# Local attention layers: the turned keys are copied from PSUM by ScalarE instead of VectorE

## The chip, the cores and the metric

The kernel runs on one core of a Trainium2 chip. The core has five engines, each with its own instruction queue: TensorE (PE; its weight loads are shown as PEld and overlap the matmuls), VectorE (DVE), ScalarE (ACT), GpSimd (POOL) and SyncE (SP, which here issues the DMAs). An engine runs its queue in order; where it needs another engine's result it waits on a semaphore, and all that is queued behind the waiting instruction waits too. The metric is the device time of one execution in microseconds (us), lower is better.

## The reference

A two-block network on x[4, 1024, 128], all in fp32. Block 0 is a feature attention and a mixture of experts. Block 1 is a windowed attention with 16 heads, followed by two "local layers" (DEPTH 2, HEADS 8, DIM_HEAD 64, WINDOW 64). The change lies in the local layers:

```
def local_attention(q, k, v):                  # 8 heads of 64
    bq = q in windows of 64, times 8
    bk, bv = look_around(k), look_around(v)    # a window and the one before it: 128 keys
    sim = einsum('bhwid,bhwjd->bhwij', bq, bk)
    sim = where(mask, -max, sim)               # i < j, i > j + 64, before the start
    return einsum('bhwij,bhwjd->bhwid', softmax(sim), bv)

def _layer(x, wqkv, qs, ksc, wo, lg, lb, w1, b1, w2, b2):
    q, k, v = split(shift_token(x) @ wqkv)     # 3 x 512 columns
    q, k = l2norm(q) * qs, l2norm(k) * ksc
    q, k = rotary_xpos(q, k)
    x = x + local_attention(q, k, v) @ wo
    h = layernorm(shift_token(x)) * lg + lb
    a, g = split(h @ w1 + b1)                  # 2 x 341 columns
    return x + (a * gelu(g)) @ w2 + b2
```

## The kernel before

The local layers are cut into 64 tiles of 128 tokens: 2 layers, 4 batches, 8 tiles each; (l, b, t) names one. Activations are kept transposed (features on partitions). One loop over `g` (from -1 to 67) runs all 64 tiles as a software pipeline: an iteration works on several tiles at different stages. Its body in the order in which it is written, which is also TensorE's order, since the surrounding pool block schedules TensorE by hand (`manual_schedule` with PE alone):

1. `scores(g)`, L885: 32 small matmuls of the turned keys `kT` and queries `qT` into two PSUM tiles `s`. VectorE then applies mask, scale and row minimum for the eight heads (L892, "pr").
2. `project(g+2, 0)`, L653: the query product `qk` in PSUM. ScalarE squares it (`sq`, L656); VectorE makes `co` (L658), `si` (L663) and the square sums `ss` (L665); POOL adds `co` and `si` (L673).
3. `flip(g-2, 0)`, L926: the first half of the probabilities is transposed (`ptr`); ScalarE copies it out (`pt`, L928).
4. `over_sums(g-1)`: the probabilities are divided by their sums. VectorE takes the reciprocal of `sm` (L912); the product `pr` times `sm` is L919 on POOL for the first half of the heads, and L919 on VectorE for the second half. For the five tiles with (l, b) = (0, 0) and t from 3 on, called `light`, the second half is four activations on ScalarE (L917).
5. `project(g+2, 1)`: the same for the keys; POOL also makes the norms (L668, L669) and scales `co` by them (L675).
6. `flip(g-2, 1)`, and `exps(g)`: eight exponentials on ScalarE (L904), whose sums over a row are `sm`.
7. `turn(g+1, 0)`, L845 (L849 for light tiles): four transposes of the query's `co` into the PSUM tile `qktr`; ScalarE copies them out as `qT` (L852).
8. `outputs(g-3)`, L940: probabilities times values into the PSUM tile `o`; ScalarE copies it out (`os`, L944).
9. `turn(g+1, 1)`: the same transposes for the keys' `co`; VectorE copies them to `kT` (L858).
10. The first side step of the iteration, `values(g-1)` (L864, copied out by ScalarE as `vs`, L866), `project_out` in every fourth iteration (`yp`, L951; added up by VectorE, L952), and the other side steps.

The side steps are the MLP of an earlier half batch: `mlp_in` (transposes L972 and statistics), `mlp_out` (L160, `hn` L161 on ScalarE), `mlp_gate` (three products `gm` L986, Gelu on ScalarE L990), `mlp_up` (three products `a` L995, VectorE L997), `mlp_down` (`ym` L1003, VectorE L1004). They return with a period of four iterations: one with `mlp_down`, one with `project_out` and `mlp_out`, one with `mlp_gate`, one with `mlp_up` and the next `mlp_in`. Gelu and the exponential need different activation tables, so ScalarE loads a table (ACT_TABLE_LOAD, at L990 and L904) on each side of the gate.

PSUM has eight banks here: two for `s` (pool `pS`) and six (pool `pM`, tag "mid") that `qk`, `ptr`, `qktr`, `o`, `v`, `yp`, `gm`, `a`, `ym` and the rest take in turn. A tile that takes a bank waits until what read the bank's previous content is done, which may be an engine that has nothing to do with the tile itself.

The order of VectorE's, ScalarE's and POOL's instructions is not written by hand: the framework's scheduler decides it. `tc.issue_after(x)` (L911) keeps the instructions of its block behind instruction x in that order; in `over_sums` it names the `kT` copy that was issued last before it in the program.

Of the kernel before, what the change touches and what calls it, by code (L numbers as in the profile page):

```python
# [22 lines left out]
ALU = mybir.AluOpType  # L23
AX = mybir.AxisListType
PSUM = bass.MemoryType.PSUM

P = 128
# [21 lines left out]
def adaln_blocks(ctx: ExitStack, tc: tile.TileContext, a: dict, out: bass.AP):  # L49
    nc = tc.nc  # L50
    pe, act, dve, pool = nc.tensor, nc.scalar, nc.vector, nc.gpsimd
# [11 lines left out]
    def bc(ap, shape):  # L63

        return ap.unsqueeze(len(ap.shape)).to_broadcast(shape)
# [219 lines left out]
    with (  # L285
# [7 lines left out]
        kept = {}  # L293
# [306 lines left out]
    def const1(name, shape):  # L600
        return c1.tile(shape, F32, tag=name, name=name)

    wl = []
    for l in range(DEPTH):
        w = [const1(f"wqkv_{l}", [P, 3, HEADS * DH]), const1(f"wo_{l}", [P, 4, D]), const1(f"w1_{l}", [P, 2 * HID]), const1(f"w2_{l}", [P, 3, D])]
# [38 lines left out]
    late = {}  # L644
    pj = ctx.enter_context(tc.tile_pool(name="pj", bufs=3))

    def project(l, b, t, w, ps):


        nt = f"{l}_{b}_{t}_{w}"  # L650
        if w == 0:
            late[l, b, t, "ss"] = pj.tile([P, 2, HEADS], F32, tag="ss", name=f"ss_{nt}", bufs=4)
        pe.matmul(ps, lhsT=hs[l, b][:, t * P : (t + 1) * P], rhs=wl[l][0][:, w, :], start=True, stop=True)  # L653
        ph = ps.rearrange("p (h e) -> p h e", e=DH)
        sq = pj.tile([P, HEADS, DH], F32, tag="sq", name=f"sq_{nt}", bufs=2)
        act.activation(sq, ph, AF.Square)  # L656
        co = pj.tile([P, HEADS, DH], F32, tag=f"co{w}", name=f"co_{nt}")
        dve.tensor_tensor(co, ph, abs_[l][:, 0, t, w, :].unsqueeze(1).to_broadcast([P, HEADS, DH]), ALU.mult)  # L658
        si = pj.tile([P, HEADS, DH], F32, tag="si", name=f"si_{nt}", bufs=3)

        ex = bass.AP(tensor=ps.tensor, offset=ps.offset + 32, ap=[ps.ap[0], [DH, HEADS], [-32, 2], [1, 32]])
        sn = abs_[l][:, 1, t, w, :].rearrange("p (i e) -> p i e", i=2).unsqueeze(1).to_broadcast([P, HEADS, 2, 32])
        dve.tensor_tensor(si.rearrange("p h (i e) -> p h i e", i=2), ex, sn, ALU.mult)  # L663
        ss = late[l, b, t, "ss"]
        dve.tensor_reduce(ss[:, w, :], sq, AX.X, ALU.add)  # L665
        if w == 1:

            pool.tensor_scalar(ss, ss, 1.0e-24, None, ALU.max)  # L668
            pool.tensor_tensor(ss, ss, nhalf[:, 0:2].unsqueeze(2).to_broadcast([P, 2, HEADS]), ALU.pow)  # L669
        if w == 0 and light(l, b, t):  # L670
            late[l, b, t, "si"] = si
        else:
            pool.tensor_tensor(co, co, si, ALU.add)  # L673
        if w == 1:
            pool.tensor_tensor(co, co, bc(ss[:, 1, :], [P, HEADS, DH]), ALU.mult)  # L675
        late[l, b, t, "co", w] = co

    def light(l, b, t):

        return (l, b) == (0, 0) and t >= EARLY  # L680
# [5 lines left out]
    with (  # L686
# [107 lines left out]
        for g in range(-1, NG8 + 2):  # L794
            b, t = divmod(g, NT)
            ahead = 0 <= b and b + 1 < B
            if g == -1:
                weights(0, 0)
            when(g + 2, scores)
            when(g + 2, weights)  # L800
            if ahead and t in (2, 4):
                queries(b + 1, t // 2 - 1)
            for after, k, f in ((6, 0, tokens), (8, 0, normed), (11, 1, tokens), (13, 1, normed)):
                if (g - after) % NT == 0 and 0 <= (g - after) // NT < B - 1:
                    f((g - after) // NT, k, "h3")
            for at, k, f in ((1, 0, tokens), (3, 0, normed), (5, 1, tokens), (7, 1, normed)):
                if g == at:
                    f(B - 1, k, "h2")
            when(g - 1, back)
            when(g + 1, flip, (0, 1))  # L810
            when(g + 1, values)
            when(g, outputs)
            when(g + 1, flip, (2, 3))
            if t == 5 and 0 < b <= DEPTH:
                rotary(tab, abs_[b - 1], b - 1)
            if g % 4 == 1 and g > 4:
                project_out((g - 5) // NT, (g - 5) % NT // 4)
            if ahead and t in (3, 5):
                keys(b + 1, t // 2 - 1)

            for i, w in ((0, 0), (0, 1), (1, 0), (1, 1), (2, 0), (2, 1))[max(0, g - NG8 + 6) : max(0, g - NG8 + 7)]:
                project(0, 0, i, w, ps.tile([P, BLK], F32, tag="t", name=f"qk_0_0_{i}_{w}", bufs=2))
# [6 lines left out]
    with (  # L829
# [6 lines left out]
        kept = late  # L836

        def turn(l, b, t, w):
            nt = f"{l}_{b}_{t}_{w}"
            co = kept.pop((l, b, t, "co", w)).rearrange("p h e -> p (h e)")  # L840
            tp = pM.tile([P, 4, P], F32, tag="mid", name=f"qktr_{nt}")
            si = kept.pop((l, b, t, "si"), None) if w == 0 else None
            for i in range(4):
                if si is None:
                    pe.transpose(tp[:, i, :], co[:, i * P : (i + 1) * P], ident)  # L845
                else:

                    for j, x in enumerate((co, si.rearrange("p h e -> p (h e)"))):
                        pe.matmul(tp[:, i, :], lhsT=x[:, i * P : (i + 1) * P], rhs=ident, start=(j == 0), stop=(j == 1))  # L849
            if w == 0:  # L850
                kept[l, b, t, "q"] = wp.tile([P, 4, P], F32, tag="qT", name=f"qT_{nt}")
                act.copy(kept[l, b, t, "q"], tp)  # L852
                return
            if t == 0:

                kept[l, b, "k"] = wb.tile([P, 4, 64 + N], F32, tag="kT", name=f"kT_{nt}", bufs=1)
                pool.memset(kept[l, b, "k"][:, :, 0:64], 0.0)
            kept["copied"] = dve.tensor_copy(kept[l, b, "k"][:, :, 64 + t * P : 64 + (t + 1) * P], tp)  # L858

        def values(l, b, t):  # L860

# [45 lines left out]
        def over_sums(l, b, t):  # L907

            sm = kept.pop((l, b, t, "sm"))

            with tc.issue_after(kept["copied"].ins):  # L911
                dve.reciprocal(sm, sm)  # L912
                for j, eng in ((0, pool), (1, act if light(l, b, t) else dve)):
                    pr, _ = kept[l, b, t, "pr", j]
                    if eng is act:
                        for c in range(4):
                            act.activation(pr[:, c, :], pr[:, c, :], AF.Identity, scale=sm[:, j, c : c + 1])  # L917
                    else:
                        eng.tensor_tensor(pr, pr, bc(sm[:, j, :], [P, 4, P]), ALU.mult)  # L919
# [140 lines left out]
        def project_mid(l, b, t, w):  # L1060
            if (l, b) != (0, 0) or t >= EARLY:
                project(l, b, t, w, pM.tile([P, BLK], F32, tag="mid", name=f"qk_{l}_{b}_{t}_{w}"))

        for g in range(-1, tiles + 4):
# [5 lines left out]
            if 1 < g < NT - 1:  # L1070
                when(g + 1, turn, 0)
            when(g - 2, flip, 0)
            when(g - 1, over_sums)
            when(g + 2, project_mid, 1)
            when(g - 2, flip, 1)
            when(g, exps)
            for i in turns:
                if not 1 < g < NT - 1:
                    when(i, turn, 0)
                if i < EARLY and g < EARLY:  # L1080
                    when(i, turn, 1)
# [142 lines left out]
```

## Time and profile before

| what | value |
|---|---|
| time, median of 3 runs | 1245.24 us (1244.97, 1245.24, 1251.0) |
| the profiled execution | 1246.33 us, span 1244.5 us, granted TensorE clock 0.983 |
| `kT` copy, VectorE L858 | 64 of 128x512, median 0.679 us, from 580.4 to 1189.3 us |
| `qT` copy, ScalarE L852 | 64 of 128x512, median 0.577 us |
| normalising product L919 | POOL 64, median 1.042 us; VectorE 59, median 0.725 us |
| L917 on ScalarE | 20 of 128x128, median 0.390 us, from 609.8 to 644.3 us |
| reciprocal L912, VectorE | 64, median 0.186 us |
| who waits for the `kT` copy | PEld `v` L864 12.1 us in 13 waits; PEld `s` L885 6.3 us in 5; PE `s` L885 6.1 us in 16 |

The local layers' score matmuls run from 581 to 1193 us of the span; what lies before belongs to the other blocks. A line of the timeline gives start, duration, engine, source line, operation, output and inputs; the bracket at its end is how long the engine stood idle before it and which instruction ended that. The waits are summed by the waiting line and the line that ended them: us in total, times, longest. A PEld wait is one of a weight load, which can lie beside matmuls that still run; a PE wait is one of the matmul itself.

### The profile page before, as it was taken

How to read it: one execution, taken by the hardware profiler on the slowest of the kernel's cores; microseconds unless marked ns; L12 is line 12 of the kernel's file. 1: busy time of each engine (PE TensorE's matmuls, PEld its weight loads, DVE VectorE, ACT ScalarE, POOL GpSimd, SP SyncE). 2: the span in 40 equal slices, each digit the busy share in tenths (PEclk: the TensorE clock that was granted, in tenths of full speed). 3: DMA queues.
4: the chain of work that ended last, by engine and by line, in shares of the span. 5: the costliest groups of instructions: out<-in, count | busy, mean ns of one | idle time of the engine just before them, and what ended most of it. 6: DMA issues, size and time to landing. Idle time of an engine off the chain costs nothing.

```text
span 1244.5 us, 34772 instructions
## 1 busy us (share of the span) xinstructions
PE 1162.8 (93%) x13578; PEld 714.7 (57%) x13578; DVE 878.8 (71%) x2798; ACT 817.8 (66%) x2223; POOL 823.3 (66%) x813
## 2 busy tenths in 40 slices
PE   6789999999899999988898999999999999999998
PEld 5644453534476667755665556665555556565564
DVE  5556263452476667666878988898898888998864
ACT  3363373322577677766886788788877887788862
POOL 4436445746334445444889988888899889888840
PEclk8699999999999999999999999999999999999999
DMA  6040404021400000000112111111111111111110
GB/s 179 1 130 8 138 0 132 7 74 63 137 4 4 3 20 14 11 3 3 35 27 48 27 35 26 32 40 27 39 28 34 39 29 45 38 27 31 36 40 26
DMA packets 36136, 51.04 MB, mean 41 GB/s; under 512 B 5850, under 2 KB 17668, under 8 KB 35844
## 3 DMA queue, kind: packets, MB, share of 16 engines
q1 hardware_dynamic: 35540, 48.29, 14.1%
q8 instruction: 107, 1.75, 0.6%
q10 hardware_dynamic: 432, 0.53, 0.1%
q14 instruction: 57, 0.47, 0.1%
HBM read 26.52 MB, written 2.36 MB: 23 GB/s over the span
## 4 chain that ended last, share of the span: by engine, by line
PE 43%; DVE 27%; ACT 18%; POOL 7%; issue 5%; DMA 1%; POOLq 0%; ACTq 0%; SPq 0%; DVEq 0%
ACT pr L904 5%; PE h L489 4%; PE yp L951 4%; DVE pr L892 3%; DVE co L658 3%; PE s L885 3%; DVE si L663 3%; DVE ss L665 3%; PE ptr L735 3%; PE qk L653 3%; POOL u L494 2%; ACT sq L656 2%; PE s L261 2%; PE obank L752 2%; DVE ge L997 2%
## 5 line engine op out<-in xcount | busy, mean ns | idle before, releaser
L904 ACT ACTIVATE pr<-pr,mx 128x128 f32<-128x128 f32 x512 | 200.8, 403 | 88.2 <-DVE mx L892 88.1
L673 POOL TENSOR_TENSOR co<-co,si 128x512 f32<-128x512 f32 x123 | 156.7, 1280 | 79.5 <-DVE si L663 72.2
L669 POOL TENSOR_TENSOR ss<-ss,nhalf 128x16 f32<-128x16 f32 x64 | 191.7, 2995 | 5.3
L892 DVE CUSTOM_DVE_ANT_0 pr<-s,masks,ss 128x128 f32<-128x128 f32 x512 | 144.2, 342 | 42.4 <-PE s L885 42.0
L653 PE MATMUL qk<-wqkv,hs 128*128 128x512 f32 x256 | 137.7, 620 | 4.9 <-ACT pt L737 4.9
L494 POOL TENSOR_TENSOR u<-u,cw 128x512 f32<-128x512 f32 x64 | 81.1, 1271 | 74.4 <-ACT u L492 74.4
L489 PE MATMUL h<-hT,w 128*128 128x512 f32 x256 | 123.8, 605 | 4.0 <-DVE g L496 4.0
L496 DVE TENSOR_TENSOR g<-u,h 128x512 f32<-128x512 f32 x64 | 43.8, 686 | 114.9 <-POOL u L494 114.9
L279 DVE TENSOR_REDUCE mx<-s 128x4 f32<-128x448 f32 x128 | 73.5, 617 | 56.4 <-PE s L270 56.4
L658 DVE TENSOR_TENSOR co<-qk,ab 128x512 f32<-128x512 f32 x128 | 86.7, 677 | 26.0 <-ACT sq L656 26.0
L904 ACT ACTIVATION_READ_ACCUMULATOR pr<-pr,mx 128x1 f32 x512 | 101.7, 199 | 0.0
L492 ACT ACTIVATE u<-h 128x512 f32<-128x512 f32 x64 | 38.2, 598 | 93.2 <-PE h L489 85.7
L926 PEld LDWEIGHTS ptr<-ident,pr 128*128 128x128 f32 x512 | 63.5, 141 | 61.6 <-issue 54.8
L663 DVE TENSOR_TENSOR si<-qk,ab 128x512 f32<-128x512 f32 x128 | 86.8, 678 | 0.0
L489 PEld LDWEIGHTS h<-hT,w 128*128 128x128 f32 x256 | 48.3, 194 | 66.2 <-issue 51.0
L665 DVE TENSOR_REDUCE ss<-sq 128x8 f32<-128x512 f32 x128 | 86.2, 673 | 0.0
L656 ACT ACTIVATE sq<-qk 128x512 f32<-128x512 f32 x128 | 74.9, 586 | 14.8 <-PE qk L653 12.3
L845 PE MATMUL qktr<-ident,co 128*128 128x128 f32 x492 | 76.9, 280 | 6.6 <-POOL co L675 5.3
L885 PEld LDWEIGHTS s<-kT,qT 64*64 64x64 f32 x2048 | 56.8, 134 | 45.6 <-issue 22.1
L919 POOL TENSOR_TENSOR pr<-pr,sm 128x512 f32<-128x512 f32 x64 | 74.7, 1168 | 7.9 <-DVE sm L912 7.9
L885 PE MATMUL s<-kT,qT 64*64 64x128 f32 x2048 | 72.1, 277 | 7.6 <-DVE kT L858 6.1
L737 ACT COPY pt<-ptr 112x512 f32<-112x512 f32 x128 | 72.5, 612 | 8.6 <-PE ptr L735 8.6
(212 smaller groups left out, 2871.2 us busy)
## 6 DMA issues: line engine op xcount, KB each, us to landing
cw<-cd SPq DMA_DIRECT2D x128, 128.0 KB, 3.0
ve<-vs SPq DMA_DIRECT2D x120, 128.0 KB, 2.3
hs<-hT SPq DMA_DIRECT2D x16, 256.0 KB, 3.2
out<-out SPq DMA_DIRECT2D x7, 256.0 KB, 2.7
xin<-in_x SPq DMA_DIRECT2D x3, 512.0 KB, 6.1
w<-in_w SPq DMA_DIRECT2D x3, 512.0 KB, 5.0
wqkv<-in_wqkv SPq DMA_DIRECT2D x2, 768.0 KB, 5.3
ab<-in_tab SPq DMA_DIRECT2D x1, 1024.0 KB, 7.3
```

The source lines that it names most:

```text
L489: pe.matmul(h, lhsT=w[:, c * P : (c + 1) * P], rhs=hT[b][:, blk(k)], start=True, stop=True)
L494: pool.tensor_tensor(u, u, kept[b, k, "cw"][:, c, :], ALU.mult)
L653: pe.matmul(ps, lhsT=hs[l, b][:, t * P : (t + 1) * P], rhs=wl[l][0][:, w, :], start=True, stop=True)
L656: act.activation(sq, ph, AF.Square)
L658: dve.tensor_tensor(co, ph, abs_[l][:, 0, t, w, :].unsqueeze(1).to_broadcast([P, HEADS, DH]), ALU.mult)
L663: dve.tensor_tensor(si.rearrange("p h (i e) -> p h i e", i=2), ex, sn, ALU.mult)
L665: dve.tensor_reduce(ss[:, w, :], sq, AX.X, ALU.add)
L669: pool.tensor_tensor(ss, ss, nhalf[:, 0:2].unsqueeze(2).to_broadcast([P, 2, HEADS]), ALU.pow)
L673: pool.tensor_tensor(co, co, si, ALU.add)
L885: pe.matmul(S[j][qs, c, :], lhsT=q[rw, c, qs], rhs=k[rw, c, at : at + P], start=True, stop=True)
L892: dve.tensor_tensor_reduce(out=pr[:, c, :], in0=S[j][:, c, :], in1=mk[:, min(t, 1), :], scale=kept[l, b, t, "ss"][:, 0, h : h + 1], scalar ...
L904: act.activation(pr[:, c, :], pr[:, c, :], AF.Exp, bias=mx[:, j, c : c + 1], scale=-1.0, accum_out=sm[:, j, c : c + 1])
```

## The change

Three lines change. The keys' copy from PSUM goes from VectorE to ScalarE, in all 64 tiles. It was also the instruction behind which `over_sums` was kept; that place is taken by the last square sum (L665) that `project` issued before it in the program. In the loop body `over_sums(g-1)` follows `project(g+2, 0)`, so that is the query's square sum of the same iteration, where before it was the `kT` copy of the iteration before. Nothing of what is computed changes.

```
@@ project
         ss = late[l, b, t, "ss"]
-        dve.tensor_reduce(ss[:, w, :], sq, AX.X, ALU.add)
+        late["summed"] = dve.tensor_reduce(ss[:, w, :], sq, AX.X, ALU.add)
@@ turn
-            kept["copied"] = dve.tensor_copy(kept[l, b, "k"][:, :, 64 + t * P : 64 + (t + 1) * P], tp)
+            act.copy(kept[l, b, "k"][:, :, 64 + t * P : 64 + (t + 1) * P], tp)
@@ over_sums
-            with tc.issue_after(kept["copied"].ins):
+            with tc.issue_after(kept["summed"].ins):
```

(`kept` and `late` are the same dictionary.)

## The prediction

> **What bounds the kernel now.** I read the busy times first, then stretches of the steady part, then its waits, then single iterations.
>
> ```profile
> PE 1162.8 (93%) x13578; PEld 714.7 (57%) x13578; DVE 878.8 (71%) x2798; ACT 817.8 (66%) x2223; POOL 823.3 (66%) x813
> ```
>
> The window view of one stretch of the local layers (start:end, length, then busy us and instructions of PE, PEld, DVE, ACT, POOL, then clock, DMA share, GB/s):
>
> ```profile
> 800.00:900.00 100.00, 99.38 (x957) 59.86 (x955) 83.98 (x290) 79.88 (x243) 86.73 (x71) 1.00 0.15 36
> ```
>
> TensorE leaves 0.62 us of 100 open, so whatever makes it wait lengthens the kernel, and there is little waiting to take away. The local layers run in a cycle of four iterations of 39.84 us (score groups start at 784.4, 794.1, 804.8, 814.2 and 824.2); I name them by their side step: D (down), P (project_out), G (gate), U (up and mlp_in). From about 682 to 1200 us there are 13 cycles. The waits between 700 and 1180 us that touch the change:
>
> ```profile
> PEld v L864 <- DVE kT L858: 11.1, 12, 1.0
> DVE co L658 <- ACT sq L656: 9.6, 12, 1.0
> PEld a L995 <- DVE si L663: 6.8, 12, 0.6
> ...
> PE s L885 <- DVE kT L858: 2.8, 11, 0.3
> ```
>
> Each comes once a cycle. Two name the copy that moves; the third says that in U the last up product's weights already wait for VectorE's `si`, so anything put ahead of that `si` is paid in full. The iteration U, from the timeline (start, us, engine, line):
>
> ```profile
> 811.45 0.58 ACT L852 COPY qT<-qktr 128x512 f32<-128x512 f32 x1
> 811.91 0.59 ACT L944 COPY os<-o 128x512 f32<-128x512 f32 x1
> 812.52 1.28 ACT L990 ACT_TABLE_LOAD   x1
> ...
> 818.45 0.69 DVE L658 TENSOR_TENSOR co<-qk,ab 128x512 f32<-128x512 f32 x1 [0.78 <-ACT sq L656]
> ...
> 821.58 0.28 PEld L995 LDWEIGHTS a<-hn,w 128*85 128x85 f32 x2 [0.54 <-DVE si L663]
> ...
> 822.04 0.68 DVE L858 COPY kT<-qktr 128x512 f32<-128x512 f32 x1
> 822.77 0.30 PEld L864 LDWEIGHTS v<-wqkv,hs 128*128 128x128 f32 x2 [0.91 <-DVE kT L858]
> ```
>
> ScalarE runs from `os` at 811.91 through the table load, three Gelus, `vs`, the second table load and the first exponential to the square at 817.84 without a pause; VectorE stands idle 0.78 us for that square, then runs six products and sums and `kT`. So U hangs on ScalarE, then VectorE, then TensorE.
>
> **The change part by part.** It takes 64 copies of 0.678 us off VectorE (43.4 us busy) and adds 64 to ScalarE, which I price by the same shape and PSUM source there, `qT` L852: 0.576 us each, 0.47 from its start to the next (811.45 to 811.91). The changed program's own instruction order then says where the rest goes. The ScalarE copy stands behind `os`, and ahead of the table load in G. The reciprocal L912 moves up behind the first square sum of an iteration, and VectorE's normalising product L919 behind the second `co`: both ahead of the second `si`. POOL's L919 moves behind the first `co` sum. In D that order exists already and gives the prices:
>
> ```profile
> 790.74 0.18 DVE L912 RECIPROCAL sm<-sm 128x8 f32<-128x8 f32 x1
> 790.85 0.63 DVE L658 TENSOR_TENSOR co<-qk,ab 128x512 f32<-128x512 f32 x1
> 791.40 0.78 DVE L919 TENSOR_TENSOR pr<-pr,sm 128x512 f32<-128x512 f32 x1
> ...
> 792.11 0.68 DVE L663 TENSOR_TENSOR si<-qk,ab 128x512 f32<-128x512 f32 x1
> ```
>
> Start to start, the reciprocal takes 0.11 and the product 0.71.
>
> *U, a loss.* The copy in G pushes ScalarE's solid run by 0.47, so U's square and VectorE's first product come 0.47 later; the reciprocal and L919 add 0.82 ahead of the second `si`. That `si` (820.85, 0.68 long) ends 0.47+0.82 = 1.29 later, at 822.81 in place of 821.52, and the last up product's weights, 0.06 behind it today, go from 821.58 to 822.87. Its matmuls were not late today (0.43 is a pass, weights at 820.41 and 820.84; 819.98 plus four of them is 821.70, 0.12 after the weight load); the `v` matmul behind them was, by 0.21 (819.98 plus six of 0.43 is 822.56, and it ran at 822.77, when `kT` was done). So `v`, `mlp_in` and the next scores come 1.29-0.21 = 1.07 later (rounded rows). Times 13: +13.9. Bounds: 0.61 (8 us) if the 0.47 on ScalarE finds cover, 1.29 (17 us) if `v` then finds another wait of its own. I take 1.07 because every piece has its own row. Behind `v` stands all of the next iteration, so nothing hides it. `kT` itself ends on ScalarE at about 824.4 (`os` 823.4, copy 823.9), ahead of scores due 825.3.
>
> *D, a gain.* The scores' wait for `kT` (0.29 at 794.12) goes: ScalarE's `os` begins at 791.96, its copy ends near 793.0, and scores can't start before `v` is through at 793.83 or so. Worth 0.25 (2.8 us over 11 waits), times 13: -3.3. Bounds 0 and -0.29.
>
> *P, a small loss.* After the change project_out's PSUM tile waits for `qT` in place of VectorE's work; `qT` runs from 800.80 to 801.38 and the first matmul L951 runs at 801.25 today. If only the matmul waits it is 0.13, if its weights (0.19) wait too some 0.34: I take 0.25, as today's wait there stands on the weights. Times 13: +3.3, bounds +1.7 and +4.4.
>
> *G, nothing.* Its PSUM tiles wait for the first `si` (809.51), `qT` (812.03) and `os` (812.50), each before its use (810.62, 812.34, 813.20); `kT` near 813.0 is before scores at 814.15.
>
> *The first batch, a loss.* For five tiles ("light") the second half of the product is four ScalarE activations L917. Today they lie in a gap:
>
> ```profile
> 616.76 0.58 ACT L944 COPY os<-o 128x512 f32<-128x512 f32 x1
> 617.86 0.59 ACT L866 COPY vs<-v 128x512 f32<-128x512 f32 x1 [0.52 <-PE v L864]
> 618.34 1.28 ACT L917 ACTIVATE pr<-pr,sm 128x128 f32<-128x128 f32 x4
> ```
>
> After the change they stand amid the exponentials, ahead of `os` and `kT`. There the loop is scores at 609.62, first exponential 1.66 later, `os` 5.48 after that. With 1.28 more, 0.47 to the copy, 0.58 of copy and 0.05 to scores it is 9.52 against 8.56: +0.96 for three iterations, +2.9. The iterations around it, by the same sums, give -0.3, +1.5, +0.4 and about -0.7: +0.9. Bounds for the batch: 0 (the four hide in a VectorE wait) to +6.
>
> The relief of VectorE elsewhere buys nothing: its 84 of 100 us leave slack that TensorE (99.4) sets. Nor does a DMA move.
>
> The sum: 13.9-3.3+3.3+3.8 = +17.7. The profiled run took 1246.33 (span 1244.5), 1.1 over the median; on the median 1245.24 that is 1263. All low ends: 8-3.8+1.7+0 = +6; all high: 17+0+4.4+6 = +27.
>
> The Trainium skill (Perfetto Trace Analysis, Identifying the Most-Contended Engine) speaks for the change: for engines other than TensorE occupancy is a fair measure, and the fullest is to be relieved first. By that VectorE, above ScalarE in the window view, should be unloaded, and if all 43.4 us counted the kernel would take some 1202, an estimate. The rows above go against it, since in U VectorE waits for ScalarE.
>
> **The rivals.** (1) Not slower: the copy's waits on TensorE are all that counts, and the moved 0.82 is covered by VectorE's 0.78 idle before U's first product. Place: U. It decides if the second `si` ends no more than some 0.1 later than now (matmuls due 821.70). Then 13 times 0.21+0.25 is won, 6.0, and 1.7 lost in P: 1241. Against it: the built order puts the moved pair behind that idle time. (2) Little change: U's lateness only replaces the 0.21, D's gain pays P, and the first batch's 3.8 stays: 1249. For it speaks the 0.91 that the `v` weights wait today; against it that this is weight time, of which only 0.21 reaches the matmul. (3) POOL turns late: its L919 (1.04) behind the `co` sum holds up the chain to L675, whose result is at 798.77 for a turn at 799.46 in P. 1.04-0.69 = 0.35 times 13 is 4.6 more: 1267. Against it: POOL takes the same work and in D this order today.
>
> **How the numbers follow.** Forecast 0.62, rival 1 0.13, rival 2 0.17, rival 3 0.08. The time is the forecast's, 1263; its own range, the sums of low and of high ends, is 1251 to 1272. For 8 in 10 it reaches down over rival 2 and leaves out rival 1 and the top, where all high ends would have to meet: 1247 to 1270. A change under 0.5% (6.2 us: 1239 to 1251.5) can't be told from none. Faster: half of rival 1, 0.07. Same: the other half and most of rival 2, 0.18. Slower: 0.75.
>
> **What would show it.** In the profile after: `a` L995 waiting for `si` some 1.3 to 1.8 us in U, not 0.54; no wait of scores for `kT` in D; the cycle 39.84 growing to about 40.9; `yp` waiting for `qT`; periods of 9.5 in place of 8.56 near 610 to 635; VectorE's busy time down by 43. Wrong if U's second `si` isn't late, or if scores wait for ScalarE's `kT` in the steady part.

## The result and the profile after

The changed kernel takes 1258.74 us (median of 6 runs, 1254.94 to 1261.91) against 1245.58 us for the kernel before (6 runs, 1244.14 to 1251.0): a ratio of 1.0098, 95% interval [1.0072, 1.0123]. That is slower by some 12 to 13 us, about 1%, and clear of the 0.5% that the forecast used as its bound. The profiled run took 1258.30 us, span 1256.5, clock 0.983 as before.

The busy times of the kernel after:

```profile
PE 1168.4 (93%) x13578; PEld 714.8 (57%) x13578; DVE 847.1 (67%) x2734; ACT 847.5 (67%) x2287; POOL 822.5 (65%) x813
```

The window view from 800 to 900 us of the kernel after, columns as in the prediction:

```profile
800.00:900.00 100.00, 98.66 (x932) 58.47 (x934) 78.59 (x277) 82.30 (x254) 86.28 (x71) 1.00 0.14 32
```

VectorE lost 31.7 us of work and ScalarE gained 29.7; the engines are now level at 847, and the kernel is slower. The place to look is what TensorE waits for. The waits of the kernel after between 700 and 1180 us (waiting line, what ended the wait: us in total, times, longest):

```profile
PEld a L995 <- DVE si L663: 20.8, 24, 1.4
...
DVE co L658 <- ACT sq L656: 15.0, 12, 1.3
...
PEld yp L951 <- ACT qT L852: 9.4, 12, 0.9
...
PE a L995 <- DVE si L663: 6.6, 12, 0.6
PEld v L864 <- ACT qT L852: 6.2, 12, 0.6
```

The scores' wait for `kT` is gone, as forecast. In its place the weights of the up products wait for `si` three times as long as before (20.8 against 6.8), and now the matmul itself waits too (6.6), VectorE waits longer for the square (15.0 against 9.6), and `yp` and `v` wait for `qT`. The cycle of four iterations grew from 39.8 to 40.6 us (40.9 was forecast).

Period of each iteration, from one score group's first matmul to the next one's (median of 11 cycles), of all kernels of this study; "light" is the middle one of the three light iterations, and "layers" the time from the first score group to the last. Each ratio is that to runs of the kernel before taken alongside:

| kernel | D | P | G | U | light | layers | ratio to before, 95% interval |
|---|---|---|---|---|---|---|---|
| before | 9.67 | 10.66 | 9.37 | 10.08 | 8.57 | 610.97 | |
| after | 9.37 | 10.93 | 9.37 | 10.96 | 9.42 | 625.03 | 1.0098 [1.0072, 1.0123] |
| move_only | 10.05 | 10.91 | 9.37 | 10.49 | 8.57 | 625.15 | 1.0092 [1.0055, 1.0128] |
| copy_only | 9.37 | 10.66 | 9.37 | 10.86 | 8.26 | 615.60 | 1.0035 [1.0010, 1.0060] |
| copy_u_and_d | 9.37 | 10.66 | 9.37 | 10.38 | 8.26 | 609.54 | 0.9997 [0.9976, 1.0017] |
| light_as_before | 9.37 | 10.93 | 9.37 | 10.97 | 8.26 | 621.06 | 1.0072 [1.0051, 1.0094] |
| g_copy_on_vectore | 9.37 | 10.92 | 9.37 | 10.47 | 9.42 | 618.21 | one run |
| after_q_early | 9.37 | 11.09 | 9.37 | 10.38 | 9.42 | 620.27 | 1.0085 [1.0057, 1.0114] |
| before_q_early | 9.87 | 10.66 | 9.37 | 9.80 | 8.57 | 607.67 | 0.9961 [0.9943, 0.9979] |
| u_and_d_q_early | 9.37 | 10.79 | 9.37 | 9.89 | 8.26 | 604.00 | 0.9944 [0.9918, 0.9969] |
| d_only_q_early | 9.37 | 11.01 | 9.37 | 9.78 | 8.57 | 606.01 | 0.9949 [0.9929, 0.9968] |
| d_and_first_q_early | 9.37 | 11.01 | 9.37 | 9.79 | 8.26 | 605.32 | 0.9946 [0.9923, 0.9969] |
| copy_all_q_early | 9.37 | 10.78 | 9.37 | 10.36 | 8.26 | 610.51 | 1.0003 [0.9980, 1.0025] |

Between before and after the layers differ by 14.06 us; the spans differ by 12.0, because the first score group began 2.09 earlier in the profile after. That start lay anywhere from 575.9 to 581.4 us in these thirteen profiles, in which each engine runs the same instructions in the same order up to 570 us, so it is scatter from one execution to the next, and the column "layers" shows an effect of 1 us better than one run's time does.

### The profile page after: what moved, and what is told of

It reads as the page before. It is cut to its first block, busy times and chain, and to the rows that moved or that the text cites. A ratio compares the mean times of both kernels' runs of the same rounds, so it can differ in the third digit from the quotient of the medians.

```text
span 1256.5 us, 34784 instructions
## 1 busy us (share of the span) xinstructions
PE 1168.4 (93%) x13578; PEld 714.8 (57%) x13578; DVE 847.1 (67%) x2734; ACT 847.5 (67%) x2287; POOL 822.5 (65%) x813
## 4 chain that ended last, share of the span: by engine, by line
PE 58%; ACT 15%; DVE 15%; POOL 7%; issue 5%; DMA 1%; POOLq 0%; ACTq 0%; SPq 0%; DVEq 0%
PE qk L653 5%; PE yp L951 5%; PE h L489 5%; PE s L885 4%; PE v L864 3%; PE gm L986 3%; PE o L940 3%; PE qktr L845 3%; PE ptr L735 3%; PE ym L1003 3%; ACT pr L904 3%; PE ptr L926 2%; PE s L261 2%; POOL u L494 2%; ACT ge L990 2%
## 5 line engine op out<-in xcount | busy, mean ns | idle before, releaser
L673 POOL TENSOR_TENSOR co<-co,si 128x512 f32<-128x512 f32 x123 | 156.7, 1274 | 86.9 <-DVE si L663 83.6
L669 POOL TENSOR_TENSOR ss<-ss,nhalf 128x16 f32<-128x16 f32 x64 | 187.1, 2924 | 5.3
L919 POOL TENSOR_TENSOR pr<-pr,sm 128x512 f32<-128x512 f32 x64 | 88.0, 1375 | 16.4 <-DVE sm L912 12.0
L665 DVE TENSOR_REDUCE ss<-sq 128x8 f32<-128x512 f32 x128 | 86.1, 672 | 0.0
```

## The experiments

"The pair" is the reciprocal L912 with the normalising products behind it (L919, in light tiles also L917). Of each edit the lines that matter are shown; `[...]` and `(...)` stand for what did not change, and where only new lines stand, they replace the line of the same purpose.

### The two halves of the change apart

*move_only*: the order of the pair changes, the copy stays on VectorE (edit of the changed kernel).

```
-            act.copy(kept[l, b, "k"][...], tp)
+            dve.tensor_copy(kept[l, b, "k"][...], tp)
```

> VectorE keeps the keys' copy; only the reciprocal and the normalising products are moved ahead of the second si, as in the changed kernel. Theory (the moved pair is most of the loss): in U the second si ends 0.71 later (the pair's spacing measured in the changed kernel), the copy behind it too, so v waits for the copy and the period of U grows by 0.6 to 0.7 and that of P by 0.1 to 0.3 (yp behind the later si); D and G as before; the three light iterations stay near 8.6, since ScalarE's os is later but the copy on VectorE is not. Sum over 13 cycles some +9 to +12: 1255 to 1258 against 1245.5. Rival (the copy on ScalarE is the loss, the moved pair is covered by VectorE's idle time): U at 10.08, 1245 to 1247.

Measured: 1257.67 us (6 runs), the layers as long as with the whole change. U grew by 0.41, less than the 0.6 to 0.7 expected, P by 0.25, and D by 0.38, which no theory had: the time lies in the expected 1255 to 1258 only because D, and 1.4 us in the first batch, made up for what U lacked. The three largest waits of TensorE's matmuls (700 to 1180 us):

```profile
PE a L995 <- DVE si L663: 5.6, 12, 0.5
PE s L885 <- DVE kT L858: 3.6, 6, 0.6
PE s L885 <- ACT vs L866: 3.3, 5, 0.7
```

The moved pair alone makes the up products wait for `si`, and D's scores wait longer for `kT` and `vs`. It is no free part of the change. `v` does not wait for the copy here, as the theory had it: its weights and those of `yp` wait for `qT` (6.2 and 10.3 us, 12 waits each).

*copy_only*: ScalarE copies, the pair stays behind the copy (edit of the kernel before).

```
-            kept["copied"] = dve.tensor_copy(kept[l, b, "k"][...], tp)
+            kept["copied"] = act.copy(kept[l, b, "k"][...], tp)
```

> ScalarE makes the keys' copy in all 64 tiles; the reciprocal and products stay behind that copy, as before the change. Theory: U has only the 0.47 of the copy ahead of the gate's table load and no longer waits for VectorE's copy, so its period is 10.1 to 10.3 (before 10.08, changed 10.89); D loses 0.3 (9.37), P gains 0.25 (10.92), G 9.37; the light iterations fall to 8.3 to 8.6 (changed 9.42). Sum +0 to +4: 1245 to 1249. Open: in U VectorE's product now stands behind the statistics and could delay the next row minima in D by up to 0.7. Rival (ScalarE's copy is the loss): U near 10.9, 1256 or more.

Measured: 1248.37 us (10 runs). D, G and the light iterations as expected, but U 10.86, where 10.1 to 10.3 was expected, and P unchanged at 10.66, where +0.25 was expected. The timeline of U in this kernel says why (start, us, engine, line):

```profile
817.66 0.68 DVE L663 TENSOR_TENSOR si<-qk,ab 128x512 f32<-128x512 f32 x1
...
819.26 0.58 ACT L852 COPY qT<-qktr 128x512 f32<-128x512 f32 x1
...
819.89 1.13 PE L864 MATMUL v<-wqkv,hs 128*128 128x512 f32 x2 [0.40 <-ACT qT L852]
```

The second `si` is done at 818.34, in good time; what `v` waits for is `qT`, which ScalarE copies only behind all its exponentials. `v` reads nothing of `qT`, so what it waits for is its PSUM bank. By the waits, in the kernel before `v` took the bank that VectorE's `kT` copy frees; here it takes the one that `qT` frees. (The profile shows the waits, not the bank numbers.) Nobody wrote that: no edit names a bank, yet the engine that `v` or `yp` waits for changes from kernel to kernel. With `yp` in P it is the other way round: after the change it takes `qT`'s bank, here it keeps the one that `si` frees (2.9 us in 12 waits of its weights), and P stays at 10.66.

### The copy where it gains, and the price of the bank

*copy_u_and_d*: as copy_only, in U and D alone.

```
+            to = act.copy if t % 4 >= 2 else dve.tensor_copy
+            kept["copied"] = to(kept[l, b, "k"][...], tp)
```

> ScalarE makes the copy only in the iterations U and D (tiles with t mod 4 of 2 and 3), VectorE in P and G; the pair stays behind the copy as before. Theory: nothing is put ahead of the gate's table load and nothing ahead of si, so U falls by its 0.2 wait for the copy (9.9), D by 0.3 (9.37), P (10.66) and G (9.37) stay: 13 times -0.5, some 1239. If VectorE's product behind the statistics in U delays D's row minima and with them D's exponentials and outputs, D grows by up to 0.7 and the sum is 1245 to 1249. Rival (any copy on ScalarE costs): over 1250.

Measured: 1244.52 us (10 runs), no difference from the kernel before that can be told. D gained its 0.30; U lost 0.30 where a gain was expected, although nothing is ahead of the table load or of `si` here. `v` waits 4.0 us in 11 matmuls for `qT` in this kernel too. Up to `v`, TensorE, the squares and both `si` in U run as in the kernel before, to within 0.02 us; there `kT` is done 8.57 us after the scores, here `qT` at 8.87. So 0.30 is the price of the bank alone.

*g_copy_on_vectore*: the changed kernel, G's copy back on VectorE.

```
+            to = dve.tensor_copy if t % 4 == 1 else act.copy
+            to(kept[l, b, "k"][...], tp)
```

> The changed kernel with the copy of iteration G left on VectorE, so that ScalarE's table load in G is not pushed. Theory: U's square, qT and si come 0.47 earlier, the pair alone is left ahead of the second si, v some 9.1 after the scores: U 10.4 to 10.5 in place of 10.89; D, P and G as in the changed kernel (9.37, 10.92, 9.37). Some 5 us less than the changed kernel. Rival (the pair alone makes U's loss): U stays near 10.9.

Measured in a single run (1248.46 us): U 10.47 (from 10.96), the rest of the cycle as in the changed kernel, the layers 6.8 us shorter. With the pair in its new place, the copy ahead of the table load is worth 0.49 in U.

*after_q_early*: the changed kernel, with the queries' turn ahead of the exponentials.

```
+            if g >= NT - 1:
+                when(g + 1, turn, 0)
             when(g, exps)
             for i in turns:
-                if not 1 < g < NT - 1:
+                if g <= 1:
                     when(i, turn, 0)
```

> The changed kernel, with the turn of the queries written ahead of the exponentials from iteration 7 on, so that ScalarE copies qT after the second pt instead of behind all eight exponentials; TensorE's order is the same. Theory (U is set by which PSUM bank v and the last up product get, and when its reader is done): the banks are dealt anew, the last up product takes the one that qT frees early and v the one that the second si frees, 8.6 after the scores; U falls from 10.89 to 9.9 to 10.1 although the copy, the pair and their order on VectorE stay. D 9.37. The time: 13 times -0.8 to -1.0, some 1246 to 1249. Rival (VectorE's late second si or ScalarE's full queue holds U whatever the bank): U stays over 10.6, 1255 or more.

Measured: U 10.38, two thirds of its loss gone with the copy, the pair and their order on VectorE in place. The second `si` ends some 8.6 us after the scores, as in the changed kernel: the loss is no late VectorE as such, but which bank hangs on it. The timeline of U there:

```profile
821.85 0.68 DVE L663 TENSOR_TENSOR si<-qk,ab 128x512 f32<-128x512 f32 x1
...
822.58 0.36 PEld L864 LDWEIGHTS v<-wqkv,hs 128*128 128x128 f32 x2 [0.53 <-DVE si L663]
822.75 1.02 PE L864 MATMUL v<-wqkv,hs 128*128 128x512 f32 x2
```

`v` now takes `si`'s bank and the last up product waits for neither. It is not the 9.9 to 10.1 expected: the first up product still starts 0.30 late, behind the late first `si`, and the scores then wait for ScalarE's `kT`, which ends 10.33 us after the scores before. From 700 to 1180 us:

```profile
PEld s L885 <- ACT kT L858: 9.3, 17, 0.8
```

P grew to 11.09, where TensorE's turn waits for POOL (5.0 us in 12 waits). The time, 1255.56 us over only 4 runs from 1251.24 to 1259.88, misses the 1246 to 1249 expected and can't be told from the changed kernel's; the layers, 4.8 us shorter, can.

### The first batch

*light_as_before*: the changed kernel, with the old place of the pair for the five light tiles.

```
+            kept["copied"] = act.copy(...)
+            with tc.issue_after(kept["copied" if light(l, b, t) else "summed"].ins):
```

> The changed kernel, but for the five light tiles the pair (L912, L917) stays behind the copy, as before the change. Theory (the four activations L917 amid the exponentials are what the first batch loses): the three light iterations 8.2 to 8.6 in place of 9.42 and the one of 9.40 back to 7.9 to 8.3; the steady cycle unchanged at 40.5; some 4 us less than the changed kernel: 1254 to 1255. Rival (the copy on ScalarE is what costs there): light iterations stay at 9.1 or more, no change in time.

Measured: 1255.10 us (9 runs), the layers 3.97 us shorter than after, the light iterations at 8.26. ScalarE's timeline in a light iteration, first of the changed kernel:

```profile
613.62 0.58 ACT L928 COPY pt<-ptr 128x512 f32<-128x512 f32 x1
614.09 1.29 ACT L917 ACTIVATE pr<-pr,sm 128x128 f32<-128x128 f32 x4
...
616.50 0.59 ACT L858 COPY kT<-qktr 128x512 f32<-128x512 f32 x1
```

and then of light_as_before:

```profile
616.09 0.60 ACT L858 COPY kT<-qktr 128x512 f32<-128x512 f32 x1
616.57 0.42 ACT L917 ACTIVATE pr<-pr,sm 128x128 f32<-128x128 f32 x1
...
617.34 1.01 ACT L917 ACTIVATE pr<-pr,sm 128x128 f32<-128x128 f32 x3
```

Behind the copy the four activations cost nothing: no matmul shows a wait in these three iterations, while in the changed kernel the scores' matmuls wait 1.2 us in each for ScalarE's `kT`. Ahead of it they cost 1.16 (9.42-8.26). The copy itself gains 0.31 here (8.57-8.26).

### Versions that beat both kernels

*before_q_early*: the early turn alone, in the kernel before. *u_and_d_q_early*: with the copy of copy_u_and_d.

> The kernel before with the same early turn of the queries, no copy moved. Theory: v no longer waits for VectorE's kT (its bank now comes from the second si, done 7.4 after the scores): U 9.85 to 9.95 in place of 10.08; D keeps its wait of scores for kT (9.7). Sum some -2 to -3: 1242 to 1243. Rival (the early copy pushes exponentials and what waits for them): no gain, 1245 or more.

> ScalarE copies the keys in U and D only, and the queries' turn is early. Theory: U 9.8 to 9.9, since v waits neither for kT nor for qT; D 9.37; P 10.66 and G 9.37 as before: 13 times -0.5 to -0.6, some 1237 to 1239, faster than the kernel before. Rival (gains are given back in D, where row minima come later): cycle 39.8, 1244 to 1246.

Measured: 1239.68 us (10 runs) and 1237.88 us (8 runs), both faster than the kernel before. U falls to 9.80 (9.85 to 9.95 was expected) and 9.89, as expected; the wait of D's scores for `kT` grows in the first (D 9.87, where 9.7 was expected) and is gone in the second, whose P grew to 10.79 where 10.66 was expected.

*d_only_q_early* (`t % 4 == 3`), *d_and_first_q_early* (`t % 4 == 3 or (l, b) == (0, 0)`), *copy_all_q_early* (copy_only with the early turn):

> ScalarE copies the keys in iteration D alone (tiles with t mod 4 of 3), the queries' turn is early. Theory: U 9.80 as with the early turn alone, D 9.37 as wherever ScalarE copies, P near 10.66 and G 9.37: a cycle of 39.2 to 39.3 against 39.8, 13 times -0.6, some 1236 to 1238, faster than the kernel before. Rival (D's gain is given back in P, where POOL's co for the turn comes late): P 10.8 to 11.0, cycle 39.5, 1239 to 1241.

> As d_only_q_early, with ScalarE's copy also in all tiles of the first batch. Theory: the light iterations go from 8.57 to 8.26 and the two behind the batch lose their wait for kT, some 1 us less than d_only_q_early: 1235 to 1237. Rival (ScalarE is what the first batch hangs on): 1 us more.

> The copy on ScalarE in all 64 tiles, the pair left behind the copy as before the change, the queries' turn early. Theory: the copy as such costs only U's first up product, which waits for a si 0.47 later: U 10.0 to 10.2 (copy alone 10.86), D 9.37, P 10.66 to 10.8, G 9.37; some -2 to -4, 1240 to 1243. Rival (ScalarE can't take 64 copies whatever the banks): U over 10.6, 1247 or more.

Measured: 1239.39 (12 runs), 1239.17 (9) and 1246.11 us (10). In the first of them P gave back what D gained, and the time came out in its rival's 1239 to 1241; TensorE's only wait of its own in that kernel, 700 to 1180 us:

```profile
PE qktr L845 <- POOL co L675: 3.9, 12, 0.6
```

ScalarE's copy in the first batch gained 0.7 us of layers, too little for the times to show (1235 to 1237 was expected). The copy in all tiles missed its U (10.36, expected 10.0 to 10.2) and comes out even. Set beside after_q_early it says more: there the pair lies ahead of the second `si`, here behind the copy, so that this `si` ends 0.75 us earlier; yet `v` starts at the same time after the scores (8.81 and 8.80) and U is the same (10.38 and 10.36). With the queries' turn early the pair's place costs a steady U nothing; what is left there is the copy's 0.47 in ScalarE's queue, by the late first up product and by `kT`. What the pair still costs after_q_early lies in P and in the first batch (4.3 and 4.6 us of layers). The intervals of the four faster versions overlap; by the layers u_and_d_q_early is the shortest, 7.0 us under the kernel before.

## Why the prediction was right, and where it was not

The forecast was slower by 17.7; the layers of the two profiles differ by 14.1, the medians by 13.2. Its terms, with the sums of the measured differences of the same iterations (how many in brackets; the range from 682 to 1200 us holds 12 of D and P, not 13):

| term (U, D, P, G: from score group 12 on, counted from 0, but for the last) | forecast | measured |
|---|---|---|
| U | +13.9 (13) | +10.8 (13) |
| D | -3.3 (13) | -3.8 (12) |
| P | +3.3 (13) | +2.0 (12) |
| G | 0 | +0.4 (13) |
| first batch, score groups 0 to 10 | +3.8 | +4.1 |
| score group 11 and the last | none | +0.6 |

**U: the term that was mis-sized.** The chain forecast is there, piece by piece. The timeline of G's end and of U, kernel after:

```profile
816.77 0.60 ACT L858 COPY kT<-qktr 128x512 f32<-128x512 f32 x1
...
817.39 1.28 ACT L990 ACT_TABLE_LOAD   x1
...
823.31 0.69 DVE L658 TENSOR_TENSOR co<-qk,ab 128x512 f32<-128x512 f32 x1 [1.25 <-ACT sq L656]
...
825.11 0.19 DVE L912 RECIPROCAL sm<-sm 128x8 f32<-128x8 f32 x1
...
825.77 0.73 DVE L919 TENSOR_TENSOR pr<-pr,sm 128x512 f32<-128x512 f32 x1
...
826.42 0.68 DVE L663 TENSOR_TENSOR si<-qk,ab 128x512 f32<-128x512 f32 x1
...
827.16 1.09 PE L995 MATMUL a<-hn,w 128*85 128x512 f32 x2 [0.52 <-DVE si L663]
...
827.30 0.58 ACT L852 COPY qT<-qktr 128x512 f32<-128x512 f32 x1
...
827.93 0.34 PEld L864 LDWEIGHTS v<-wqkv,hs 128*128 128x128 f32 x2 [0.55 <-ACT qT L852]
828.09 1.02 PE L864 MATMUL v<-wqkv,hs 128*128 128x512 f32 x2
```

The copy stands ahead of the table load, VectorE's idle time before the first `co` grows by 0.47 (0.78 to 1.25), and the pair lies ahead of the second `si`. The forecast put that `si` 1.29 later; counted from the scores it is 1.18 (827.10-818.54 against 821.53-814.15). The missing 0.11 is the pair, which took 0.71, not 0.82: D's row showed the second `co` giving way after 0.55, not 0.60, and the prediction charged the product's full 0.71, which is 0.65 here. `v` came 0.93 later (1.07 forecast), and from `v` to the next scores this U needs 0.11 less than before, so that it grew by 0.82, the median U by 0.88.

The larger gap is in the reason. The prediction saw one wait decide U; there are two, less than 0.2 apart. The last up product starts at 827.16, behind `si`; after its two passes of 0.43 `v` could run at 828.02. In the row above `v`'s weights wait for `qT`, done at 827.88, and `v` runs at 828.09. By copy_only the wait for `qT` alone makes U 10.86, of the 10.96 with both. The pair without G's copy, through `si`, makes 10.47 (g_copy_on_vectore). So 0.47 on ScalarE counted not only because it makes `si` late: either of two queues carries it to TensorE. Taking the pair out of U, the remedy that the prediction's sum suggests, wins back 0.10 (copy_only). The prediction named the possibility, `v` finding "another wait of its own", as its upper bound, but not `qT`.

**D.** 9.37 wherever ScalarE copies in D, in ten kernels: the wait for `kT` was the whole of it, and slightly more than the 0.25 taken.

**P.** `yp` waits for `qT` with its weights, as the built order said. Kernel after:

```profile
804.90 0.58 ACT L852 COPY qT<-qktr 128x512 f32<-128x512 f32 x1
...
805.54 0.30 PEld L951 LDWEIGHTS yp<-os,wo 128*128 128x128 f32 x2 [0.83 <-ACT qT L852]
```

0.25 was right for most cycles (0.26 or 0.27 in seven of the twelve, 0.16 or 0.17 in four; one of -0.45 makes the sum smaller). What it belongs to was not asked: move_only has it without the copy (10.91, `yp` waiting for `qT` there too), copy_only lacks it. It comes with the pair's move, which changes the bank that `yp` takes.

**The first batch.** +0.85 for each light iteration against 0.96; for those behind them +1.50 against 1.5, +0.49 against 0.4, -0.64 against -0.7. The prediction doesn't say which iteration its -0.3 is of; the one ahead of the light ones lost 0.49. Right by its own steps, but for +0.60 in score group 2, which was not forecast and stays unexplained.

**The rivals.** Rival 1 (covered by VectorE's idle time) fell with the 1.25 above: the idle time moved with the square. Rival 2 had U's lateness replace the 0.21; U lost 0.88. Rival 3 did not happen here: in a P of the kernel after (scores at 798.25) the keys' turn is where it was, 5.34 us after the scores, and POOL's `co`, though 0.45 later, is done at 5.10. A wait of the same place appeared in another kernel: with the early turn and D's copy, POOL's `co` holds the turn in P, and P rises from 10.66 to 11.01. That this is the 0.35 which the prediction worked out is chance, as POOL's product stands in D where it stood in the kernel before.

**The rule weighed.** Perfetto Trace Analysis, Identifying the Most-Contended Engine, of the Trainium skill would relieve the fullest engine first. VectorE was that engine, TensorE apart, over the whole span (878.8 us against POOL's 823.3); in the prediction's own window view it was not, POOL was fuller (86.73 against 83.98). VectorE was relieved by 31.7 us and the kernel lost 13; copy_only, the relief with the least around it, lost 0.35% [0.10, 0.60]. What decided was the waits of single matmuls, above all in one iteration of four.

**TensorE's share.** The prediction read from 99.38 us busy of 100 that little waiting was left to take away. u_and_d_q_early took 0.36 us from a cycle of 39.8, 0.9%. The row of a 128x512 matmul pass lasts 0.59 us where the next pass starts 0.43 after it, so a wait of up to 0.16 between two passes shows as no idle time: the busy share hid part of the waiting.

## What to carry to other kernels

Price an edit at the wait it shifts, and then look for the second wait behind it: where two queues reach the same matmul within a few tenths, undoing one of them gives nearly nothing back. An edit near the copies out of PSUM can change which bank a matmul takes: read from the waits whose bank each matmul takes, and let what is copied out early be freed early. Moving `qT` ahead of the exponentials gained 3.3 us of layers, the moved copy in U and D alone 1.4, both together 7.0. An "issue after" anchor that moves along with an edit is an edit of its own; here it cost as much alone as the whole change.

## What was not expected of the hardware

The same normalising product took longer in its new place. Minimum, median and longest ns of L919, kernel before:

```profile
L919 POOL TENSOR_TENSOR pr<-pr,sm x64: 1034/1042/1545, 586.3 to 1198.6; 128x512 f32<-128x512 f32 x64
L919 DVE TENSOR_TENSOR pr<-pr,sm x59: 683/725/1566, 586.3 to 1198.5; 128x512 f32<-128x512 f32 x59
```

and after:

```profile
L919 POOL TENSOR_TENSOR pr<-pr,sm x64: 1029/1487/1497, 588.4 to 1210.6; 128x512 f32<-128x512 f32 x64
L919 DVE TENSOR_TENSOR pr<-pr,sm x59: 692/977/1575, 588.7 to 1210.5; 128x512 f32<-128x512 f32 x59
```

VectorE's median rose from 0.725 to 0.977 us and POOL's from 1.042 to 1.487, with the same shapes. In the new order the two run at about the same time (in the P near 804 us of the kernel after, VectorE's took 1.24 us from 804.15 and POOL's 1.49 us from 804.80). That the overlap is the cause shows most clearly on POOL, in the rows of other kernels too. In the kernel before, the 20 products that overlap VectorE's by more than 0.1 us have a median of 1.49 us, and the other 44 took 1.04 to 1.05; in copy_only these are 6 of 1.48 and 58 of 1.03 to 1.05. In these three kernels every VectorE product that took over 0.75 us began while one of POOL's 128x512 operations ran, most of them the sum L673 (the 1.24 above began while that ran, from 803.56 to 804.84). No run varied the overlap alone. The longer product is also most of why VectorE's busy time fell by 31.7 and not by the 43.4 of the copies: its L919 grew from 47.7 to 57.2 us.
